# Roots and masks of the scale blocks on GpSimd in a four-layer graph network

## The chip, the cores and the metric

The kernel runs on one NeuronCore of one Trainium2 chip. The metric is the device time of one execution in microseconds (us), the median of several runs. The core has a matrix engine (TensorE, PE in the profile), a vector engine (VectorE, DVE), an engine for activation functions (ScalarE, ACT), a programmable vector engine (GpSimd, POOL) and a queue that issues the transfers (SyncE, SP). Each engine works through its own instructions in order and waits on semaphores for the others.

## The reference

The input is 64 graphs of 256 nodes with 128 features, x of shape (64, 256, 128), and a symmetric 0/1 adjacency with a diagonal of ones, adj of shape (64, 256, 256), in float32. Four layers follow each other, each with a residual and a norm over the features:

```
x = layernorm(x + L0(x, adj))   # max over neighbours j of relu(p_i + q_j + b)
x = layernorm(x + L1(x, adj))   # elu projections, aggregated by adj and adj^T, tanh
x = layernorm(x + L2(x, adj))   # graph convolution, see below
x = layernorm(x + L3(x, adj))   # see below
```

Two places have inverse roots beside the norms. Layer 2 scales the adjacency by the degrees:

```
A_hat = adj + eye;  deg = A_hat.sum(-1);  dinv = where(deg > 0, rsqrt(deg), 0)
norm_A = dinv[:, None] * A_hat * dinv[None, :]
```

Layer 3 normalizes a message for each pair of nodes, so it has one inverse root per pair:

```
pre = m_j[None, :] + m_i[:, None] + b1                       # (i, j, feature)
msg = gelu((pre - mean) * rsqrt(var + 1e-5) * g1 + be1)      # mean, var over features
agg = (msg * adj[i, j]).sum(j)
updated = layernorm(concat(x, agg) @ W2 + b2) * g2 + be2
```

## The kernel before, in words

The work is written as generators, one set per graph. Four stages of four neighbouring graphs run together: `last` of one graph (layer 3's messages and update), `third` of the next (layer 2, and the start of layer 3), `second` (layer 1) and `first` (sorting of the edges, layer 0). `together` takes turns among the four generators: each `yield` ends a turn, and the stages have weights of 34, 34, 14 and 44 turns. All 64 graphs are unrolled. The tile framework gives each instruction a place on its engine's queue from this order and from its own plan of when operands and buffers are free, so the order on a queue is near to the order in the code, not equal to it. The transfers all go through SP's queue.

Layer 3 works on edges alone. The edges of a graph, sorted into 40 slots, are laid out along the free dimension, features across the 128 partitions, in 10 tiles per graph of up to 1024 edges (eight of 1024, two of 704). `sums_of` makes one tile: matmuls into `bigp` (L728), the addition of the receiving node's part into `pre` (L732), the squares (L736, ACT), a matmul with ones for their sum over the features (L743), and the mean square plus eps as one row (L745, ACT). The row goes by DMA to a line in DRAM (L750). After every second tile, a group, the line is read back as a block `vr` of up to 128 partitions x 16 elements (L762), and a mask of the filled places as `fu` (L764); `inverse_root` makes 1/sqrt of the block (L74 on ACT, L75 on DVE), the mask is multiplied in (L769, DVE), and the block goes out to `scale_line` (L771). `last` fetches the scales of a tile two tiles ahead, broadcast to all partitions, as `rs_s` (L828), multiplies `pre` by them (L839, DVE), takes the Gelu (L841, ACT) and adds the message into the sums of the nodes (`fold`, L492). `sums_of` runs four tiles ahead of this.

There are 64 x 5 = 320 blocks `vr`. `inverse_root` serves two more places: `dinv` of layer 2, 128x2, once per graph (the degrees, L271 to L274; first used at L293), and `rs` of the norms, 128x2, five times per graph: in `layernorm` the variance plus eps (L174), a yield, the root, a yield, and the application (L180, or L184 and L185).

[...] an ACT_TABLE_LOAD stands before each change of set. Sqrt, Gelu (L841) and Exp (L194, L198, the elu) need different sets; squares, copies and the like need no load of their own.

Of the kernel before, what the change touches and what calls it, by code (L numbers as in the profile page):

```python
# [9 lines left out]
F32 = mybir.dt.float32  # L10
BF16 = mybir.dt.bfloat16
AF = mybir.ActivationFunctionType
ALU = mybir.AluOpType
# [6 lines left out]
P = 128  # L20
EPS = 1e-5
# [22 lines left out]
def kernel(  # L44
# [9 lines left out]
    nc = tc.nc  # L54
# [5 lines left out]
    consts = ctx.enter_context(tc.tile_pool(name="consts", bufs=1))  # L60
# [6 lines left out]
    eps_t = consts.tile([P, 1], F32, name="eps_t")  # L67
    nc.vector.memset(eps_t, EPS)
    minus1 = consts.tile([P, 1], F32, name="minus1")
    nc.vector.memset(minus1, -1.0)  # L70

    def inverse_root(t):

        nc.scalar.activation(t, t, AF.Sqrt)  # L74
        nc.vector.reciprocal(t, t)  # L75

    def load(src, shape, name):
        t = consts.tile(shape, F32, name=name)
# [43 lines left out]
    with tc.tile_pool(name="prep", bufs=1) as prep, tc.tile_pool(  # L122
        name="ps_prep", bufs=2, space=bass.MemoryType.PSUM
# [33 lines left out]
    class Shared:  # L157
# [5 lines left out]
        def psum(self):  # L163
            return self.ps_mm.tile([P, 512], F32, name="mm")

        def layernorm(self, dst, src, g=None, be=None):

            st = self.work.tile([P, H, 6], F32, name="st", bufs=4)
            mv = self.work.tile([P, H, 2], F32, name="mv", bufs=4)
            for h in range(H):  # L170
                nc.vector.bn_stats(st[:, h], src[:, h])
                nc.vector.bn_aggr(mv[:, h], st[:, h])
            rs = self.work.tile([P, H], F32, name="rs", bufs=4)
            nc.vector.tensor_scalar(rs, mv[:, :, 1], EPS, None, ALU.add)  # L174
            yield
            inverse_root(rs)
            yield
            for h in range(H):
                if g is None:
                    nc.vector.tensor_scalar(  # L180
                        dst[:, h], src[:, h], mv[:, h, 0:1], rs[:, h:h + 1], ALU.subtract, ALU.mult
                    )
                else:
                    nc.vector.scalar_tensor_tensor(dst[:, h], src[:, h], mv[:, h, 0:1], g, ALU.subtract, ALU.mult)  # L184
                    nc.vector.scalar_tensor_tensor(dst[:, h], dst[:, h], rs[:, h:h + 1], be, ALU.mult, ALU.add)  # L185
# [75 lines left out]
        def layer_2(self, s, aT, deg_of):  # L261
# [8 lines left out]
            dinv = work.tile([P, H], F32, name="dinv")  # L270
            nc.vector.tensor_scalar(dinv, deg, 1e-30, None, ALU.max)  # L271
            inverse_root(dinv)
            yield
            nc.vector.tensor_mul(dinv, dinv, pos)  # L274
# [79 lines left out]
    def sparse(ctx):  # L354
# [35 lines left out]
        with tc.tile_pool(name="cs_prep", bufs=1) as pp:  # L390
            t = pp.tile([P, P], F32, name="upto_f")
# [4 lines left out]
            t = pp.tile([P, N], I32, name="iota_i")  # L396
            nc.gpsimd.iota(t, pattern=[[1, N]], base=0, channel_multiplier=0)
            nc.vector.tensor_copy(iota_k, t)
            t = pp.tile([P, 1], I32, name="part_i")
# [25 lines left out]
            t = pp.tile([P, 1], F32, name="gbe")  # L425
# [9 lines left out]
            for i in range(3):  # L435
                t = pp.tile([3, P], BF16, name="u_part")
# [5 lines left out]
            t = pp.tile([ROWS, g_n, g_w], F32, name="tail_f")  # L442
# [15 lines left out]
        def pieces(lo, hi):  # L458

            for s0, n, w in RECTS:  # L460
                ss = [s for s in range(s0, s0 + n) if lo <= SLOT_AT[s][0] < hi]
                if ss:
                    assert SLOT_AT[ss[-1]][0] + w <= hi
                    yield ss[0], len(ss), w, SLOT_AT[ss[0]][0] - lo

        def block(ap, n, w, at):
            return ap[:, at:at + n * w].rearrange("p (s k) -> p s k", s=n)

        def widen(ap, n):

            return ap.unsqueeze(1).broadcast_to([ap.shape[0], n, ap.shape[1]])
# [246 lines left out]
        def sums_of(s, i):  # L718

            h, t0, tl = TODO[i]  # L720
            hot, c3, dT = s["hot"], s["c3"], s["dT"]
            pre = big.tile([P, TILE], F32, name="pre", bufs=7)
            s["pre", i] = pre
            for b in range(0, tl, 512):
                bl = min(512, tl - b)
                pt = ps_big.tile([P, 512], F32, name="bigp")
                for k in range(3):
                    nc.tensor.matmul(  # L728
                        pt[:, :bl], c3[:, k, h], hot[:, h, t0 + b:t0 + b + bl], start=k == 0, stop=k == 2
                    )  # L730
                for s0, n, w, at in pieces(t0 + b, t0 + b + bl):
                    nc.vector.tensor_add(  # L732
                        block(pre[:, b:], n, w, at), block(pt, n, w, at), widen(dT[:, h, :w], n)
                    )
            sq = big.tile([P, TILE], F32, name="sq", bufs=1)
            nc.scalar.activation(sq[:, :tl], pre[:, :tl], AF.Square)  # L736
            yield

            bl = P if tl % 512 == 0 else tl // 4
            v4 = sq[:, :tl].rearrange("p (b q k) -> p b q k", q=4, k=bl)  # L740
            pr = psum()
            for q in range(4):
                nc.tensor.matmul(pr[q * Q:(q + 1) * Q, :tl // 4], ones[:, :Q], v4[:, :, q], start=True, stop=True)  # L743
            row = big.tile([P, TILE // 4], F32, name="row")
            nc.scalar.activation(row[:, :tl // 4], pr[:, :tl // 4], AF.Identity, bias=eps_t, scale=1.0 / P)  # L745
            at = sum(n for _, _, n in TODO[i - i % GROUP:i])
            if at == 0:
                s["line"] = dram.tile([1, GROUP * TILE], F32, name="line")
            line = s["line"]
            nc.sync.dma_start(  # L750
                line[:, at:at + tl].rearrange("o (b q k) -> (o q) b k", q=4, k=bl),
                row.rearrange("(q p) n -> q p n", p=Q)[:, 0, :tl // 4].rearrange("q (b k) -> q b k", k=bl),
            )
            yield
            if i % GROUP < GROUP - 1:
                return

            n = at + tl
            rows = n // PIECE
            first_at = TODO[i - GROUP + 1][0] * WIDTH + TODO[i - GROUP + 1][1]  # L760
            vr = big.tile([P, PIECE], F32, name="vr")
            nc.sync.dma_start(vr[:rows], line[:, :n].rearrange("o (p k) -> (o p) k", k=PIECE))  # L762
            fu = big.tile([P, PIECE], BF16, name="fu")
            nc.sync.dma_start(  # L764
                fu[:rows],
                s["fulls"].rearrange("h w -> (h w)")[first_at:first_at + n].rearrange("(p k) -> p k", k=PIECE),
            )
            inverse_root(vr[:rows])
            nc.vector.tensor_mul(vr[:rows], vr[:rows], fu[:rows])  # L769
            out_line = dram.tile([1, GROUP * TILE], F32, name="scale_line")  # L770
            nc.sync.dma_start(out_line[:, :n].rearrange("o (p k) -> (o p) k", k=PIECE), vr[:rows])  # L771
            at = 0
            for j in range(i - GROUP + 1, i + 1):
                s["scale", j] = out_line[:, at:at + TODO[j][2]]
                at += TODO[j][2]
            yield
# [5 lines left out]
        def third(g, s):  # L782
# [35 lines left out]
            for i in range(AHEAD):  # L818
                yield from sums_of(s, i)

        def last(g, s):
# [11 lines left out]
            for i in range(len(TODO) + 1):  # L833
                if i < len(TODO):
                    if i + AHEAD < len(TODO):
                        yield from sums_of(s, i + AHEAD)
                    h, t0, tl = TODO[i]
                    pre, rs = s.pop(("pre", i)), scale_of.pop(i)
                    nc.vector.tensor_mul(pre[:, :tl], pre[:, :tl], rs[:, :tl])  # L839
                    msgs[i] = msg = pre if t0 else big.tile([P, TILE], F32, name="sums")  # L840
                    nc.scalar.activation(msg[:, :tl], pre[:, :tl], AF.Gelu, bias=be3, scale=g3)  # L841
                    fetch(i + 2)
                    yield
# [253 lines left out]
    with tc.tile_pool(name="flag", bufs=1) as fp, tc.tile_pool(  # L1097
        name="ps_flag", bufs=1, space=bass.MemoryType.PSUM
# [44 lines left out]
```

## Time and profile before

| what | before |
|---|---|
| median of 3 runs | 5732.73 us (5721.88 to 5733.99) |
| the profiled execution, its own time | 5731.62 us |
| its span, first to last instruction | 5729.7 us |
| TensorE's mean granted clock | 0.862 of full speed |
| busy: PE, DVE, ACT, POOL | 79%, 84%, 75%, 0% of the span |

The span is read from the trace of one execution; what lies around it is 1.9 us. Busy times count instructions in execution. A group row reads: line, engine, operation, output<-input tiles with shapes, count | busy us in all, mean ns of one | idle us of the engine just before them, and what ended most of it. The chain of waits is followed back from the last instruction, at each step to what released it.

### The profile page before, as it was taken

How to read it: one execution, taken by the hardware profiler on the slowest of the kernel's cores; microseconds unless marked ns; L12 is line 12 of the kernel's file. 1: busy time of each engine (PE TensorE's matmuls, PEld its weight loads, DVE VectorE, ACT ScalarE, POOL GpSimd, SP SyncE). 2: the span in 40 equal slices, each digit the busy share in tenths (PEclk: the TensorE clock that was granted, in tenths of full speed). 3: DMA queues.
4: the chain of work that ended last, by engine and by line, in shares of the span. 5: the costliest groups of instructions: out<-in, count | busy, mean ns of one | idle time of the engine just before them, and what ended most of it. 6: DMA issues, size and time to landing. Idle time of an engine off the chain costs nothing.

```text
span 5729.7 us, 83531 instructions
## 1 busy us (share of the span) xinstructions
PE 4529.9 (79%) x27408; PEld 2508.7 (44%) x27408; DVE 4834.4 (84%) x14654; ACT 4275.2 (75%) x6485; POOL 1.9 (0%) x10
## 2 busy tenths in 40 slices
PE   5878878878778778788788788787887887877875
PEld 2444444444444444444444444444444444444443
DVE  6788888888888888888888888888888888888876
ACT  2577777777777777777777777777777777777785
POOL 0000000000000000000000000000000000000000
PEclk8888889889889889888898898898888887888986
DMA  0122222222212221221221222122212212221222
GB/s 22 44 70 63 62 63 72 62 63 66 69 57 70 65 63 63 72 63 62 63 72 62 63 65 70 59 68 65 63 62 72 64 62 63 69 66 60 68 65 74
DMA packets 292813, 365.15 MB, mean 64 GB/s; under 512 B 151952, under 2 KB 210448, under 8 KB 292368
## 3 DMA queue, kind: packets, MB, share of 16 engines
q1 hardware_dynamic: 292368, 359.73, 20.0%
q8 instruction: 217, 3.56, 0.3%
q14 instruction: 228, 1.87, 0.1%
HBM read 345.07 MB, written 14.53 MB: 63 GB/s over the span
## 4 chain that ended last, share of the span: by engine, by line
PE 52%; DVE 29%; ACT 11%; issue 4%; DMA 3%; SPq 0%; DVEq 0%; POOL 0%; ACTq 0%
PE bigp L665 11%; PE bigp L728 8%; DVE pre L839 6%; PE mm L860 5%; DVE lanes L492 4%; PE mm L743 4%; DVE hot L629 4%; DVE pre L732 4%; DVE sums L492 3%; PE bigp L681 3%; DMA rs_s<-scale_line 2%; PE mm L870 2%; PE mm L296 2%; PE mm L699 2%; PE mm L647 2%
## 5 line engine op out<-in xcount | busy, mean ns | idle before, releaser
L665 PE MATMUL bigp<-hot,q 128*128 128x512 fp8e4 (+1 forms) x3840 | 1052.3, 371 | 66.6 <-DVE lanes L492 52.6
L728 PE MATMUL bigp<-hot,c 128*128 128x512 fp8e4 (+1 forms) x3840 | 928.8, 372 | 140.2 <-DVE pre L732 140.2
L732 DVE TENSOR_TENSOR pre<-bigp,dT 128x512 f32<-128x512 f32 (+6 forms) x1664 | 846.3, 530 | 37.8 <-PE bigp L728 33.5
L492 DVE TENSOR_TENSOR lanes<-bigp,lanes 128x512 f32<-128x512 f32 (+6 forms) x1536 | 772.7, 503 | 94.6 <-PE bigp L681 86.9
L839 DVE TENSOR_TENSOR pre<-pre,rs_s 128x1024 f32<-128x1024 f32 (+1 forms) x640 | 732.9, 1150 | 48.6 <-DMA rs_s<-scale_line 48.0
L736 ACT ACTIVATE sq<-pre 128x1024 f32<-128x1024 f32 (+1 forms) x640 | 638.5, 998 | 169.9 <-DVE pre L732 163.9
L841 ACT ACT_TABLE_LOAD x535 | 686.4, 1283 | 9.5
L492 DVE TENSOR_TENSOR sums<-pre,sums 128x1024 f32<-128x1024 f32 (+6 forms) x1024 | 628.8, 614 | 41.2 <-ACT pre L841 40.7
L745 ACT ACTIVATE row<-mm,eps_t 128x256 f32<-128x256 f32 (+1 forms) x640 | 289.6, 453 | 476.9 <-PE mm L743 476.7
L841 ACT ACTIVATE pre<-pre,be,g 128x1024 f32<-128x1024 f32 (+1 forms) x512 | 594.2, 1172 | 57.8 <-DVE pre L839 53.0
L743 PE MATMUL mm<-sq,ones 128*32 128x256 f32 (+1 forms) x5120 | 482.9, 440 | 135.2 <-ACT sq L736 135.2
L74 ACT ACT_TABLE_LOAD x445 | 570.9, 1283 | 7.5
L728 PEld LDWEIGHTS <-c 128*128 128x128 bf16 x3840 | 331.2, 98 | 550.5 <-issue 136.1
L665 PEld LDWEIGHTS <-q 128*128 128x128 bf16 x3840 | 310.8, 97 | 392.6 <-issue 112.0
L296 PE MATMUL mm<-aT,hs 128*128 128x256 f32 x512 | 232.3, 600 | 316.1 <-DVE hs L293 214.8
L629 DVE TENSOR_SCALAR hot<-rank 128x512 fp8e4<-128x512 bf16 (+5 forms) x1536 | 440.5, 348 | 0.0
L681 PEld LDWEIGHTS <-pick 42*128 42x128 bf16 x2944 | 155.8, 95 | 481.5 <-issue 474.2
L296 PEld LDWEIGHTS mm<-aT,hs 128*128 128x128 f32 x512 | 135.6, 293 | 425.8 <-issue 316.1
L860 PE MATMUL mm<-w3u,sums 128*128 128x128 f32 x2048 | 296.7, 289 | 18.4 <-DVE sums L492 16.1
L194 ACT ACT_TABLE_LOAD x221 | 283.5, 1283 | 3.9
L681 PE MATMUL bigp<-lack,pick 42*128 42x36 bf16 (+16 forms) x2944 | 285.7, 187 | 0.0
L860 PEld LDWEIGHTS mm<-w3u,sums 128*128 128x128 f32 x2048 | 254.5, 195 | 37.3 <-issue 17.6
(226 smaller groups left out, 7132.6 us busy)
## 6 DMA issues: line engine op xcount, KB each, us to landing
rs_s<-scale_line SPq DMA_DIRECT2D x512, 512.0 KB
rs_s<-scale_line SPq DMA_DIRECT2D x128, 352.0 KB
an<-in_adj SPq DMA_DIRECT2D x64, 256.0 KB
x<-in_x SPq DMA_DIRECT2D x64, 128.0 KB
line<-row SPq DMA_DIRECT2D x512, 4.0 KB
out<-o SPq DMA_DIRECT2D x64, 128.0 KB
fu<-fulls SPq DMA_DIRECT2D x192, 4.0 KB
vr<-line SPq DMA_DIRECT2D x192, 8.0 KB
```

The lines of the kernel that those rows point to most:

```text
L74: nc.scalar.activation(t, t, AF.Sqrt)
L492: nc.vector.tensor_tensor(lanes[:, :k, :w], src[:, i:i + k], lanes[:, :k, :w], op)
L629: nc.vector.tensor_scalar(hot[:, :, at:at + w], rank[:, :, :w], s0 + i + 1.0 - FAR, None, ALU.is_equal, saturate=False)
L665: nc.tensor.matmul(pt[:, :tl], q3[:, i, h], hot[:, h, t0:t0 + tl], start=i == 0, stop=False)
L681: nc.tensor.matmul(o_, l_, r_, start=False, stop=i == len(todo) - 1)
L728: nc.tensor.matmul(pt[:, :bl], c3[:, k, h], hot[:, h, t0 + b:t0 + b + bl], start=k == 0, stop=k == 2)
L732: nc.vector.tensor_add(block(pre[:, b:], n, w, at), block(pt, n, w, at), widen(dT[:, h, :w], n))
L736: nc.scalar.activation(sq[:, :tl], pre[:, :tl], AF.Square)
L743: nc.tensor.matmul(pr[q * Q:(q + 1) * Q, :tl // 4], ones[:, :Q], v4[:, :, q], start=True, stop=True)
L839: nc.vector.tensor_mul(pre[:, :tl], pre[:, :tl], rs[:, :tl])
L841: nc.scalar.activation(msg[:, :tl], pre[:, :tl], AF.Gelu, bias=be3, scale=g3)
L860: nc.tensor.matmul(pt[:, cols], lanes[:, k, cols], w3u[:, 1], start=k == 0, stop=False)
```

## The change

A constant `mhalf` of 128x16 elements of -0.5 is added. `inverse_root` becomes one instruction on GpSimd: the tile to the power of `mhalf`, in place. It now serves `vr` and `dinv` only. The mask of the `vr` block is multiplied in on GpSimd, too. The mask of `dinv` (L274) stays on DVE. In `layernorm` the root stays on ACT and takes eps as its bias, so the addition of eps on DVE goes; the reciprocal on DVE now stands after the second yield, ahead of the application.

```diff
+    mhalf = consts.tile([P, 16], F32, name="mhalf")
+    nc.vector.memset(mhalf, -0.5)
+
     def inverse_root(t):
 
-        nc.scalar.activation(t, t, AF.Sqrt)
-        nc.vector.reciprocal(t, t)
+        nc.gpsimd.tensor_tensor(t, t, mhalf[:t.shape[0], :t.free_size()], ALU.pow)
...
                 nc.vector.bn_stats(st[:, h], src[:, h])
                 nc.vector.bn_aggr(mv[:, h], st[:, h])
+            yield
             rs = self.work.tile([P, H], F32, name="rs", bufs=4)
-            nc.vector.tensor_scalar(rs, mv[:, :, 1], EPS, None, ALU.add)
-            yield
-            inverse_root(rs)
-            yield
+            nc.scalar.activation(rs, mv[:, :, 1], AF.Sqrt, bias=eps_t)
+            yield
+            nc.vector.reciprocal(rs, rs)
...
             inverse_root(vr[:rows])
-            nc.vector.tensor_mul(vr[:rows], vr[:rows], fu[:rows])
+            nc.gpsimd.tensor_mul(vr[:rows], vr[:rows], fu[:rows])
```

## The prediction

> **What bounds the kernel now.** No engine is full. I read the page first, from the engines' busy time to the chain of waits and the costliest groups:
>
> ```profile
> PE 4529.9 (79%) x27408; PEld 2508.7 (44%) x27408; DVE 4834.4 (84%) x14654; ACT 4275.2 (75%) x6485; POOL 1.9 (0%) x10
> ...
> PE 52%; DVE 29%; ACT 11%; issue 4%; DMA 3%; SPq 0%; DVEq 0%; POOL 0%; ACTq 0%
> ...
> L841 ACT ACT_TABLE_LOAD x535 | 686.4, 1283 | 9.5
> ...
> L74 ACT ACT_TABLE_LOAD x445 | 570.9, 1283 | 7.5
> ...
> L194 ACT ACT_TABLE_LOAD x221 | 283.5, 1283 | 3.9
> ```
>
> The first line has busy us, share and count: three engines at 75 to 84%, GpSimd (POOL) idle. The second is the chain that ended last: PE half, DVE 29%, ACT 11%. So the three hand work to each other in a fixed order, and relief on one counts only where the chain passes it. The last three rows are ACT's loads of function tables: 535 before a Gelu, 445 before a root, 221 before an Exp; with 32 of L198 and three others 1236 loads, 1586 us, over a third of ACT's busy time.
>
> Then the groups by shape, for all that the diff touches:
>
> ```profile
> L74 ACT ACTIVATE rs<-rs 128x2 f32<-128x2 f32 x320 | 64.4, 201 | 87.9 <-DVE rs L174 85.8
> ...
> L174 DVE TENSOR_SCALAR rs<-mv 128x2 f32<-128x2 f32 x320 | 51.1, 160 | 0.1
> ...
> L75 DVE RECIPROCAL vr<-vr 128x16 f32<-128x16 f32 x192 | 47.3, 246 | 27.9 <-ACT vr L74 23.9
> ...
> L74 ACT ACTIVATE vr<-vr 128x16 f32<-128x16 f32 x192 | 40.5, 211 | 3.7 <-DMA vr<-line 2.8
> ...
> L769 DVE TENSOR_TENSOR vr<-vr,fu 128x16 f32<-128x16 f32 x192 | 31.9, 166 | 0.2
> ...
> L75 DVE RECIPROCAL vr<-vr 108x16 f32<-108x16 f32 x128 | 31.2, 243 | 1.6 <-ACT vr L74 1.5
> ...
> L74 ACT ACTIVATE vr<-vr 108x16 f32<-108x16 f32 x128 | 27.6, 216 | 1.4
> ...
> L769 DVE TENSOR_TENSOR vr<-vr,fu 108x16 f32<-108x16 f32 x128 | 21.0, 164 | 0.1
> ```
>
> These are cheap one by one. The dear part of a root is the table load ahead of it, and the reload behind.
>
> Last the list of waits, and that of the DMA queue (us, times, longest):
>
> ```profile
> DVE pre L839 <- DMA rs_s<-scale_line: 48.0, 57, 4.2
> ...
> DVE vr L75 <- ACT vr L74: 25.4, 37, 1.7
> ```
> ```profile
> SPq L771 <- DVE vr L769: 565.2, 101, 7.6
> ```
>
> The scales of a block go line, vr, root, mask, scale_line, rs_s. Whoever needs them (L839) waited for them 57 times in 640, 48 us in all: the way has slack. From the timeline, the issue of vr to the issue of the scale_line store takes 5.7 us on average, 4.4 of it until ACT begins the root. There are 320 groups, one per 17.5 us (a graph takes 87.5 us in the middle of the span).
>
> [...] around 2822 us a load starts 0.01 to 0.02 us after the instruction ahead and the next one 1.30 us after it. I use 1283. [...]
>
> **The change, part by part.**
>
> ACT loses 320 vr roots (40.5 + 27.6 = 68 us) and 64 dinv roots (64 x 0.203 = 13 us). For the loads I listed ACT's instructions in the order of the timeline and counted one wherever the set changes (Tanh being in the sets of Exp and Gelu): this gives 535 + 445 + 255 = 1235 of the 1236 there. Without these 384 roots, the same count gives 379 + 195 + 192 = 766. So some 470 fewer, x 1.283 = 603 us. The norms' roots now take eps as a bias; [...] (L745 with bias 465 ns, L692 without 366, both 128x256 from PSUM): 320 x 0.093 = +30 us. ACT: -68 - 13 - 603 + 30 = -654, to 3621 us (63%).
>
> DVE loses the adds of L174 (51.1), the reciprocals of vr (78.5) and of dinv (64 x 0.146 = 9), and the masks (52.9): -192 us, to 4642. The reciprocal of rs stays, behind the step's yield, which can only let other DVE work go first. One memset is added, once.
>
> GpSimd gets 384 powers and 320 multiplications. Lower bound of a power: its own rows of before, 0.10 us for a memset of one element and 0.45 for an affine_select of 42x192, so at least about 0.15. Upper: 17 us, where it would fill the time of a group. [...] I take 0.5 to 1 us for the likeliest case and keep the rest for the range; that is a choice, not a derivation. The multiplication I put at 0.2, between the same rows.
>
> SP's queue keeps its order of DMAs: vr (L762), fu (L764), the store (L771), the fetch (L828). Their number is unchanged. L771 now waits for GpSimd, and behind it in SP stand line<-row and rs_s. The slot of fu is freed by GpSimd's multiplication. The way of the scales gets shorter while power and mask take under about 2.8 us (5.7 less the DMA's 2.9, the shortest start of the root after the issue). On GpSimd a dinv power can stand behind a vr power whose DMA isn't there; the cover is a step's yield and the transposes and matmul ahead of L293. I put that at nothing; without the cover, 64 x some 2 us.
>
> **What of it lies on the path.** I added up the chain's pieces over the span. Root loads of L74 48.1 us in 38 pieces; next to them are 38 vr roots (7.6 us), 8 of rs and 2 of dinv, so I count four fifths of these loads for vr: -38, and -8 for the roots. Reciprocal of vr 22.0, mask 10.0: both go. L174 22.1: goes. Exp loads 89.4 + 39.7, of which 255 to 192 takes a quarter: -32. Gelu loads 12.8, 29% fewer: -4. Sum: 38 + 8 + 22 + 10 + 22 + 32 + 4 = **-136 us**. Most of ACT's 654 us lies beside other work.
>
> Not all of it comes through: PE has 52% of the chain, and what is late next is PE's own matmuls at a granted clock of 0.862. I take two thirds: -91. Against it, GpSimd's holds: I laid a hold on DVE's timeline at each vr root, and let the next two-input instruction wait for its end. A hold of 0.5 us costs DVE 48 us in all, 1 us 154, 2 us 462, 3 us 781. DVE has 1681 us of its 4834 on the chain, 35%. The likeliest case with 0.5 us and a part of the rest: 48 x 0.35 = 17, and 2 for the shorter holds of the masks: +19. Sum -72 on the profiled execution's own 5731.6 us (span 5729.7 and 1.9 around it); the median of the runs is 1.1 higher. That gives **5660 us**. Own range 5605 (all of the 136) to 5715 (a fifth of it).
>
> **Rivals.** First, the other side: **GpSimd holds the read port that VectorE needs**, at L839 (640 instructions, 733 us), the sums of L492 (1024, 629 us), L201 and the residual adds. For: DVE is the fullest engine, two-input work is about a third of its time and often queued, and nothing on its side can move away. Against: 16 elements are little to read, and the port may be let go early. Price: a power of 3 us and a mask of 0.5 cost DVE 781 + 48 = 829 us, x 0.35 = +290, less 91: +199, **5931**. It decides from where the stall is 91 / 0.35 = 260 us, a power of about 1.3 us.
>
> Second, **the power is so slow that scales come late**: at 8 us the way grows by some 6 us. If one wait per graph takes that, 64 x 6 = 384, less 91: **6025**. Against: the slack at L839.
>
> Third, **nothing comes through**: PE's throttle takes back what PE gains from waiting less, or the reordered queues lose it. Then 5725 to 5740. For: a mean clock of 0.862, in records of 1.0 and 0.5 only, means half clock for (1 - 0.862) / 0.5 = 28% of the time.
>
> That the roots don't leave ACT at all can be excluded: the diff names the engine. That the loads stay can't: norms' roots could fall where the vr roots were, one load each; at most 320 root loads instead of 195, with as many reloads, takes 250 of the 470 away and leaves the path 30 to 40 us less gain: 5695.
>
> **Chances.** Likeliest case, the loads' rival included: 0.48. Nothing: 0.11. Port: 0.31. Late scales: 0.10. About 0.2% (11 us) is what a measurement of this kernel can tell from no change. Faster 0.48, same 0.11, slower 0.41. The range goes from 5600 to 5950: the likeliest case, no change, and the port up to a power of 3 us; what is left out is the late scales, some longer holds, and a gain beyond the 136 us.
>
> **What would show it.** Right: some 770 table loads, ACT near 3620 us, DVE near 4640 with L839 still at 1216 ns and the 128x1024 sums at 1219, no vr on the chain, few waits of L771 on POOL. Wrong: two-input DVE rows grown while PSUM rows (L732, 679 ns) stay, or idle DVE time at them: the port. L839 waiting for rs_s far over 48 us: late scales. Both absent and the span unchanged: PE, with a clock below 0.862.

## The result, and the profile after

| | before | after |
|---|---|---|
| median | 5729.0 us (5721.9 to 5734.0, 4 runs) | 5932.4 us (5931.3 to 5938.1, 4 runs) |
| ratio, with 95% interval | | 1.0358 (1.034 to 1.0376) |
| the profiled execution, its span | 5729.7 us | 5929.5 us |
| granted TensorE clock | 0.862 | 0.842 |
| table loads on ACT | 1236 | 765 |
| L841's (before: L839's) wait for rs_s | 48.0 us, 57 times | 630.2 us, 137 times |

The change makes the kernel 203 us slower, 3.6%. The page of the kernel after, from its busy line, its chain and its costliest groups (line numbers are 2 or 3 higher than before):

```profile
PE 4581.4 (77%) x27408; PEld 2517.9 (42%) x27408; DVE 4706.0 (79%) x13631; ACT 3681.2 (62%) x5630; POOL 1244.0 (21%) x714
...
issue 56%; POOL 17%; PE 13%; DMA 5%; DVE 5%; ACT 2%; SPq 1%; POOLq 0%; DVEq 0%; ACTq 0%
...
L77 POOL TENSOR_TENSOR vr<-vr,mhalf 128x16 f32<-128x16 f32 (+1 forms) x320 | 1006.4, 3145 | 4463.6 <-DMA vr<-line 4463.6
L841 DVE TENSOR_TENSOR pre<-pre,rs_s 128x1024 f32<-128x1024 f32 (+1 forms) x640 | 735.1, 1149 | 630.5 <-DMA rs_s<-scale_line 630.2
...
L843 ACT ACT_TABLE_LOAD x378 | 485.0, 1283 | 6.6
```

ACT went down as intended, and the shares of PE and VectorE fell, too: all three wait more. A power takes 3.1 us. Over half of this chain is "issue", time for which the profile shows no wait, so its shares aren't laid beside those of before; the rows and the waits carry the reading. GpSimd's groups by shape:

```profile
L77 POOL TENSOR_TENSOR vr<-vr,mhalf 128x16 f32<-128x16 f32 x192 | 591.7, 3082 | 2390.6 <-DMA vr<-line 2390.6
...
L771 POOL TENSOR_TENSOR vr<-vr,fu 128x16 f32<-128x16 f32 x192 | 102.8, 536 | 15.1
L771 POOL TENSOR_TENSOR vr<-vr,fu 108x16 f32<-108x16 f32 x128 | 90.7, 708 | 10.0
L77 POOL TENSOR_TENSOR dinv<-dinv,mhalf 128x2 f32<-128x2 f32 x64 | 44.7, 698 | 149.1 <-DVE dinv L273 149.0
```

The records of GpSimd fit together: in all 320 blocks the mask begins 0.08 us after the power ends, and the store is issued 0.03 us after the mask ends. The list of waits, and under it the DMA queue's own (us in total, times, longest):

```profile
DVE pre L841 <- DMA rs_s<-scale_line: 630.2, 137, 6.9
...
DVE dinv L276 <- POOL dinv L77: 142.1, 61, 4.1
```
```profile
SPq L773 <- POOL vr L771: 1713.0, 320, 9.1
```

The last row isn't to be laid beside the 565.2 us that the prediction quotes, which is one releaser of several: before, SP stood at this store for 1251 us in all, 259 times.

The wait for the scales has grown by 582 us, and nearly all of it lies at two of the ten tiles of a graph: the third (312.9 us in 63 graphs) and the fifth (298.9 us in 63), each the first tile of its block. That is 5.0 and 4.7 us per graph. A second wait is new: VectorE's mask of the degrees (L276) waits 2.3 us, 61 times, for their power.

Two rows of VectorE decide on the first rival, that GpSimd holds VectorE up. Before:

```profile
L839 DVE TENSOR_TENSOR pre<-pre,rs_s 128x1024 f32<-128x1024 f32 x512 | 622.3, 1216 | 22.8 <-DMA rs_s<-scale_line 22.2
...
L492 DVE TENSOR_TENSOR sums<-pre,sums 128x1024 f32<-128x1024 f32 x256 | 312.0, 1219 | 37.0 <-ACT pre L841 36.9
```

And after:

```profile
L841 DVE TENSOR_TENSOR pre<-pre,rs_s 128x1024 f32<-128x1024 f32 x512 | 621.9, 1215 | 331.5 <-DMA rs_s<-scale_line 331.2
...
L494 DVE TENSOR_TENSOR sums<-pre,sums 128x1024 f32<-128x1024 f32 x256 | 311.2, 1216 | 49.2 <-ACT pre L843 49.0
```

Both have two inputs in SBUF, and take as long as before. In the trace, 70 of these 768 instructions lie wholly inside a power, with a mean of 1218 ns. So VectorE isn't locked out by a power. It is GpSimd's instructions that take longer where the two meet. A stretch of the timeline (start, duration, both in us):

```profile
2913.02 1.21 DVE L841 TENSOR_TENSOR pre<-pre,rs_s 128x1024 f32<-128x1024 f32 x1
...
2913.29 3.71 POOL L77 TENSOR_TENSOR vr<-vr,mhalf 128x16 f32<-128x16 f32 x1 [12.41 <-DMA vr<-line]
...
2917.07 1.34 POOL L771 TENSOR_TENSOR vr<-vr,fu 128x16 f32<-128x16 f32 x1
2917.12 1.21 DVE L494 TENSOR_TENSOR sums<-pre,sums 128x1024 f32<-128x1024 f32 x1
...
2918.44 0.32 SPq L773 DMA_DIRECT2D scale_line<-vr  x1
...
2923.80 1.23 DVE L841 TENSOR_TENSOR pre<-pre,rs_s 128x1024 f32<-128x1024 f32 x1 [4.55 <-DMA rs_s<-scale_line]
```

The power began while L841 ran and took 3.71 us where the shortest take 2.90. The mask met the sums of L494 and took 1.34 us where the shortest take 0.22. Then the store, the fetch, and VectorE stands 4.55 us at the next L841. Over the trace a mask that meets no multiplication of L841 and no addition into the sums takes 0.25 us on average (188), one that meets one 1.10 us (132); a power takes 2.91 us (130) and 3.30 us (190).

### The profile page after: what moved, and what is told of

Same layout as the page of the kernel before. It is cut to its first block, busy times and chain, and to the rows that moved or that the text cites. A ratio compares the mean times of both kernels' runs of the same rounds, so it can differ in the third digit from the quotient of the medians.

```text
span 5929.5 us, 82239 instructions
## 1 busy us (share of the span) xinstructions
PE 4581.4 (77%) x27408; PEld 2517.9 (42%) x27408; DVE 4706.0 (79%) x13631; ACT 3681.2 (62%) x5630; POOL 1244.0 (21%) x714
## 4 chain that ended last, share of the span: by engine, by line
issue 56%; POOL 17%; PE 13%; DMA 5%; DVE 5%; ACT 2%; SPq 1%; POOLq 0%; DVEq 0%; ACTq 0%
POOL vr L77 14%; PE bigp L667 5%; POOL vr L771 3%; DMA rs_s<-scale_line 2%; PE bigp L730 2%; DMA vr<-line 2%; PE bigp L683 1%; DVE pre L841 1%; DMA line<-row 1%; PE mm L862 1%; PE mm L745 1%; POOL dinv L77 1%; PE mm L812 1%; PE mm L701 1%; DVE lanes L494 0%
## 5 line engine op out<-in xcount | busy, mean ns | idle before, releaser
L77 POOL TENSOR_TENSOR vr<-vr,mhalf 128x16 f32<-128x16 f32 (+1 forms) x320 | 1006.4, 3145 | 4463.6 <-DMA vr<-line 4463.6
L841 DVE TENSOR_TENSOR pre<-pre,rs_s 128x1024 f32<-128x1024 f32 (+1 forms) x640 | 735.1, 1149 | 630.5 <-DMA rs_s<-scale_line 630.2
L730 PE MATMUL bigp<-hot,c 128*128 128x512 fp8e4 (+1 forms) x3840 | 940.7, 378 | 171.1 <-DVE pre L734 159.8
L494 DVE TENSOR_TENSOR lanes<-bigp,lanes 128x512 f32<-128x512 f32 (+6 forms) x1536 | 772.9, 503 | 148.9 <-PE bigp L683 144.6
L734 DVE TENSOR_TENSOR pre<-bigp,dT 128x512 f32<-128x512 f32 (+6 forms) x1664 | 831.4, 528 | 13.3 <-PE bigp L730 5.6
L494 DVE TENSOR_TENSOR sums<-pre,sums 128x1024 f32<-128x1024 f32 (+6 forms) x1024 | 626.5, 612 | 52.6 <-ACT pre L843 52.1
L745 PE MATMUL mm<-sq,ones 128*32 128x256 f32 (+1 forms) x5120 | 470.9, 446 | 197.6 <-ACT sq L738 197.6
L667 PEld LDWEIGHTS <-q 128*128 128x128 bf16 x3840 | 291.9, 98 | 402.0 <-DVE q L501 103.5
L298 PE MATMUL mm<-aT,hs 128*128 128x256 f32 x512 | 259.3, 661 | 186.7 <-DVE hs L295 186.7
L568 PE MATMUL mm<-perm,nz 128*128 128x256 bf16 x256 | 74.6, 377 | 373.8 <-DVE perm L562 373.8
L298 PEld LDWEIGHTS mm<-aT,hs 128*128 128x128 f32 x512 | 149.6, 323 | 305.1 <-issue 273.6
```

What stands on the lines that cost most here:

```text
L77: nc.gpsimd.tensor_tensor(t, t, mhalf[:t.shape[0], :t.free_size()], ALU.pow)
L494: nc.vector.tensor_tensor(lanes[:, :k, :w], src[:, i:i + k], lanes[:, :k, :w], op)
L667: nc.tensor.matmul(pt[:, :tl], q3[:, i, h], hot[:, h, t0:t0 + tl], start=i == 0, stop=False)
L730: nc.tensor.matmul(pt[:, :bl], c3[:, k, h], hot[:, h, t0 + b:t0 + b + bl], start=k == 0, stop=k == 2)
L734: nc.vector.tensor_add(block(pre[:, b:], n, w, at), block(pt, n, w, at), widen(dT[:, h, :w], n))
```

## The experiments

Each run is set against runs of the kernel before on the same chip (medians 5728 to 5730 us).

| run | median us | ratio to before, 95% interval |
|---|---|---|
| e1 power as multiplication | 5629.0 | 0.9826 (0.9809 to 0.9842) |
| e2 a second power as mask | 6589.7 | 1.1505 (1.1486 to 1.1524) |
| e3 blocks back on ACT and DVE | 5804.9 | 1.0136 (1.0119 to 1.0153) |
| e4 norms' edit alone | 5807.9 | 1.0136 (1.0119 to 1.0153) |
| e5 powers, norms as before | 5919.9 | 1.0341 (1.0324 to 1.0358) |
| e6 after, five tiles ahead | 5965.3 | 1.0413 (1.0396 to 1.0431) |
| e7 after, blocks of 128x8 | 5648.5 | 0.9856 (0.9840 to 0.9873) |
| e8 eps as bias alone | 5814.8 | 1.0155 (1.0138 to 1.0172) |
| e9 before, blocks of 128x8 | 5974.7 | 1.0433 (1.0416 to 1.0450) |
| e10 as e7, power as multiplication | 5470.6 | 0.9553 (0.9537 to 0.9569) |
| e11 blocks of 128x8, powers, norms as before | 5549.9 | 0.9690 (0.9674 to 0.9706) |
| e12 as e5, power as multiplication | 5661.8 | 0.9888 (0.9871 to 0.9904) |

**Is it the power's duration, or the new order of the queues?** e1 and e2 leave the order alone.

```diff
-    nc.vector.memset(mhalf, -0.5)
+    nc.vector.memset(mhalf, 0.0039)
...
-        nc.gpsimd.tensor_tensor(t, t, mhalf[:t.shape[0], :t.free_size()], ALU.pow)
+        nc.gpsimd.tensor_tensor(t, t, mhalf[:t.shape[0], :t.free_size()], ALU.mult)
```

> The 384 powers are multiplications by 0.0039, so neither the roots nor the values of the output are computed; every queue holds the same instructions in the same order as the changed kernel. Theory A (the power's 2.9 us stand in the way of the scales, and the order of the queues was planned for a short instruction): the block's root falls to about 0.2 us, L841's wait for rs_s from 630 to under 100 us, time 5600 to 5700. Theory B (the new order of the queues itself is bad, whatever the power takes): 5850 to 5940, with L841's wait still over 400 us. Theory C (GpSimd holds VectorE's port): falls too, but through shorter two-input rows on DVE, not through L841's wait.

```diff
-            nc.gpsimd.tensor_mul(vr[:rows], vr[:rows], fu[:rows])
+            nc.gpsimd.tensor_tensor(vr[:rows], vr[:rows], fu[:rows], ALU.pow)
```

> The mask is applied as an exponent (power in place of a multiplication), so a masked scale is 1, not 0; same order on every queue as the changed kernel, with a second power of some 2.9 us in each of the 320 groups. Theory A: the way of the scales is 2.5 us longer, two waits per graph grow by it and further tiles begin to wait: 64 x 2 x 2.5 = 320 us or more, time 6200 to 6400. Theory B: within 30 us of 5932. Theory C: up as well, by at most the 320 x 2.5 us that DVE is locked out, and the two-input rows of DVE grow by several hundred us.

GpSimd's row and the waits of e1:

```profile
L77 POOL TENSOR_TENSOR vr<-vr,mhalf 128x16 f32<-128x16 f32 x192 | 79.3, 413 | 2760.3 <-DMA vr<-line 2760.3
```
```profile
DVE pre L841 <- DMA rs_s<-scale_line: 275.2, 127, 5.2
...
DVE dinv L276 <- POOL dinv L77: 3.6, 6, 0.9
```

And those of e2:

```profile
L771 POOL TENSOR_TENSOR vr<-vr,fu 128x16 f32<-128x16 f32 x192 | 618.5, 3222 | 15.1
```
```profile
DVE pre L841 <- DMA rs_s<-scale_line: 1052.6, 203, 9.5
...
DVE dinv L276 <- POOL dinv L77: 262.0, 62, 6.4
```

In the traces of e1 and e2 every engine's instructions follow each other as in the kernel after. A multiplication of 0.4 us in the place of a power of 3.1 us gives 5629, and a power of 3.2 us in the place of a mask of 0.6 us gives 6590. Theory A holds, and B falls as the cause of the loss. From e1 to after the median rises by 303 us, 4.7 us per graph; the wait for the scales rises by 355 us and that for the degrees by 138, other waits of VectorE fall, and its idle time rises by 333 us in all. From after to e2 the median rises by 657 us, 10.3 per graph, more than was expected: beside the third and the fifth tile (305 us more) the ninth of each graph begins to wait (111.7 us), and the degrees stand behind two powers (120 us more). e1 also lets other values flow than the kernel after; in e2 only the masked scales differ, and it moves the same way. Theory C falls with the rows of VectorE above: in e2, with GpSimd busy for 2080 us, L841 at 128x1024 took 1218 ns. That one order serves both operations also shows that the planner gave the power no longer a place than a multiplication. e1 still has 275 us of the wait for the scales, where Theory A expected under 100: the order is tight even for a short root.

The traces show how tight. Call lead the time from the issue of a block's `vr` to the first multiplication that needs the block, less the wait there; the way begins at the same issue, and the part of it that the power is in ends at the issue of the store. Means over the 64 graphs, in us:

| | before | e1 | after | e2 |
|---|---|---|---|---|
| second block: lead | 12.3 | 7.5 | 7.6 | 7.7 |
| issue of `vr` to issue of the store | 4.9 | 3.2 | 6.8 | 9.5 |
| wait at the third tile | 0.0 | 1.4 | 4.9 | 7.4 |
| third block: lead | 12.5 | 7.2 | 7.2 | 7.2 |
| issue of `vr` to issue of the store | 5.9 | 4.1 | 6.3 | 8.6 |
| wait at the fifth tile | 0.4 | 2.8 | 4.7 | 6.9 |

The lead is some 5 us shorter in the new order, and the same in all three runs of it, whatever the power takes and however long SP stands at the store (829 us in e1, 2523 in e2). With the lead fixed, the wait grows as the way does.

**The edits apart.** e3 puts the blocks back (root on ACT, reciprocal and mask on DVE), e4 the degrees as well.

> The blocks' roots, reciprocals and masks are back on ScalarE and VectorE; the power of the degrees stays on GpSimd and the norms' edit stays. Theory A: the loss goes, 5690 to 5740. If the norms' edit or the degrees' power cost time, it stays above 5760. Table loads should be near 1236 again, less a few.

> Only the norms' edit: eps as the bias of the root on ScalarE, the addition on VectorE gone, the reciprocal behind the second yield; blocks and degrees as before. Expected 5690 to 5735: 51 us of DVE additions go, of which 22 us were on the chain. Against the kernel with the degrees on GpSimd as well, the difference is what 64 powers of 128x2 (0.70 us each) cost: -10 to +30 us.

Both missed: 5805 and 5808. They agree with each other, and in e3 VectorE waits for the powers of the degrees twice, 1.1 us in all: with no block's power ahead of them they are not in the way. As a price of these powers the agreement is weak, since e3 also has 122 table loads fewer than e4 (1146 against 1268). The norms' edit alone costs 78 us (e4 and e8 also keep the constant `mhalf`, unused; what that makes isn't separated). e8 takes the norms' edit apart, e5 leaves it out of the changed kernel:

```diff
             rs = self.work.tile([P, H], F32, name="rs", bufs=4)
-            nc.vector.tensor_scalar(rs, mv[:, :, 1], EPS, None, ALU.add)
             yield
-            inverse_root(rs)
+            nc.scalar.activation(rs, mv[:, :, 1], AF.Sqrt, bias=eps_t)
+            nc.vector.reciprocal(rs, rs)
             yield
```

> The kernel before with eps as the root's bias in place of the addition on VectorE, and the reciprocal right behind the root, ahead of the second yield, as before. If the reciprocal's new place made the loss of the norms' edit alone (5808), this is at 5700 to 5735; if the bias or the missing addition makes it, by the new order that the plan gives, it is near 5808.

> The changed kernel with the norms as before (addition of eps on VectorE, root and reciprocal together, then the yield); blocks and degrees keep their powers on GpSimd. Theory A (the power in the way of the scales makes the loss): still well above before, 5830 to 5950, with L841 waiting several hundred us. If the norms' edit makes a loss of its own (its run alone took 78 us more than before) that adds to it: about 5932 - 78 = 5854. If the queues' order matters most, anything from 5650 to 5950.

The place of the reciprocal is not it: e8 is at 5815. In e4 and e8 the queues are ordered anew; ACT has 1268 table loads in both instead of 1236. In the changed kernel the same edit costs 12 us (5932 against 5920). With short roots it gains 33, as e12 shows:

> As the run with the norms as before and powers on GpSimd (5920), its powers being multiplications by 0.0039, so the roots of blocks and degrees aren't computed; same order on every queue as that run. Theory A: the power's duration costs as much here as with the norms' edit, where it was 303 us: 5600 to 5640.

e12 is at 5662, 258 us under e5 with the same order, so a second order confirms the price of the power (expected were 5600 to 5640). And with e1 at 5629, the norms' edit has no fixed sign: 78, 12, -33 us. That it acts through the order that comes out is likely, but not shown; which place in the order makes the 78 us stays open.

**More lead, or a shorter way.** e6 changes `AHEAD` from 4 to 5, with 8 buffers of `pre` and 2 of `rs_s`.

> The changed kernel with tiles made five ahead instead of four (pre has 8 buffers, rs_s 2 instead of 3 to make room), so a block of scales is begun one tile earlier. Theory A: the waits at L841 for the scales fall from 630 to under 200 us, time 5640 to 5740. If the two buffers of rs_s hold the fetches up, or the order is at fault, it stays above 5800.

It is slower still, 5965, where Theory A expected 5640 to 5740. The wait for the scales did fall, from 630 to 378 us (under 200 was expected), but the order changed: 883 table loads instead of 765 (118 x 1.283 = 151 us of ACT), and powers of 128x16 that take 3.78 us on average. Whether the order or the two buffers of `rs_s` hold it up isn't separated. e7 makes the way shorter instead, with shorter powers and with no tile that waits for the second of a pair; the shares of the two aren't separated:

```diff
-        GROUP = 2
-        PIECE = 16
+        GROUP = 1
+        PIECE = 8
```

> The changed kernel with one tile to a block of scales instead of two, laid out as 128x8: 640 powers of 8 elements per partition. From the rows of the changed kernel (2.90 us for 16, 0.70 us for 2) a power of 8 should take 1.64 us; there are 3 x 320 more small transfers on SP. Theory A: the first tile of a pair doesn't wait for the second, and the way is 1.3 us shorter: waits at L841 under 300 us, time 5680 to 5800. Against it: the transfers delay each other in SP's queue, then 5900 and more.

> The kernel before with one tile to a block of scales (128x8), roots and masks on ScalarE and VectorE: the control for the changed kernel with such blocks (5648). 320 more roots, reciprocals and masks (some 0.21 + 0.23 + 0.16 us each) and up to 320 more pairs of table loads. If the smaller blocks alone made the gain, 5640 to 5700; if they help only because the power on GpSimd is shorter and begins sooner, this is slower than before, 5760 to 5900.

> The changed kernel with blocks of 128x8 and the powers as multiplications by 0.0039, so the roots aren't computed; same order on every queue as the run with blocks of 128x8 and powers (5648). It shows what 1.4 us per power still cost there. Theory A: the wait of L841 (249 us) mostly goes, 5500 to 5600. If the powers are hidden in this order, 5640 to 5650.

GpSimd's row and the wait of e7:

```profile
L77 POOL TENSOR_TENSOR vr<-vr,mhalf 128x8 f32<-128x8 f32 x512 | 962.7, 1880 | 2879.9 <-DMA vr<-line 2879.9
```
```profile
DVE pre L841 <- DMA rs_s<-scale_line: 248.8, 192, 5.1
```

The shortest power of eight elements takes 1.63 us (1.64 was worked out), the mean 1.9 us. The changed kernel gains 284 us by it, more than was expected, and is 1.4% faster than before. The same blocks with roots on ScalarE (e9) lose 4.3%, also more than was expected: 1409 table loads, ACT busy for 4524 us. So the small blocks alone don't make the gain; they pay here together with roots that need no table load. e10 shows what the powers cost even so: 178 us, with the wait down to 46.1 us without them.

> Blocks of 128x8 with powers and masks on GpSimd, the norms as before. In the changed kernel the norms' edit made 12 us (5932 against 5920 without it); so 5630 to 5670 here. In the kernel before, it made 78 us by another order of the queues; a difference of that size would again be the order.

e11 is the best version that computes everything: 5549.9 us, 3.1% faster than before. It missed the 5630 to 5670 that were expected: with these blocks the norms as before gain 99 us on e7. Another order has come out (683 table loads instead of 766); whether that is the whole of it isn't shown. Against e9, which has the same blocks and the same norms, the roots and masks on GpSimd gain 425 us. The busy line and the wait of e11:

```profile
PE 4381.6 (79%) x27408; PEld 2410.7 (43%) x27408; DVE 4745.6 (86%) x13951; ACT 3519.2 (63%) x5548; POOL 1534.5 (28%) x1354
```
```profile
DVE pre L842 <- DMA rs_s<-scale_line: 278.4, 165, 5.8
```

## Why the prediction was wrong

- **What is taken away was sized well.** 766 table loads forecast, 765 there. In the trace of before all 1236 loads stand at the first Gelu or where Sqrt, Gelu, Exp and Tanh change from one to another; none stands at the 431 repeats of one of them, nor where Tanh follows Gelu (61 times) or Exp (once). ACT -654 us forecast; the durations of its instructions add up to 648 us less. DVE -192 us forecast, 208 less in the same sum. The bias made a norm's root 93 ns longer (294 ns against 201), the 0.093 us that it was priced at; the two rows named beside that price, of L745 and L692, differ by 99 ns. The busy times fell by only 594 and 128 us, because busy time counts the overlap of neighbours once and there is less of it after. What came through to the end was taken as -91 us; e1, with a short instruction for the root, measures -101. That these two agree is in part luck: e1 contains 275 us of waits for the scales, which the -91 left out.
- **The step that failed is the duration of the power.** "I take 0.5 to 1 us for the likeliest case", the text says. It is 2.9 us at least and 3.1 on average. The text had bounds of 0.15 and 17 us and no row between; the value taken was near the lower one, and its price in the sum was +17 us, as a hold on VectorE. That a power holds VectorE was the author's assumption; no trace shows it. Measured, the power's duration costs 303 us (e1 against after), more than everything that was gained.
- **The second failed step is the slack.** "The way has slack", from 48 us of waits at L839. This is slack in the order of before, and the diff makes a new order, in which two of a graph's five blocks have 7 to 8 us of lead instead of 12 to 13. That is why the wait grew thirteenfold although the issue of `vr` to the issue of the store went from 5.69 to only 6.29 us on average over all blocks (the root starts 2.4 us after the issue, no longer 4.4), and why e1, with 3.52 us, still waits 275 us. After, the second block's scales are there 12.5 us after the issue of its `vr`; with the lead of before the wait would have been some 0.2 us in place of 4.9, an estimate from these averages. By it, the waits for the scales need both, the slow power and the shorter lead. `AHEAD` = 5 (e6) raised the two leads to 8.3 and 9.3 us only. What in the plan makes them shorter stays open.
- **A reading was off, without making the loss.** 2.9 us was taken for the shortest start of the root after the issue of `vr`, and power and mask were allowed 2.8 us. The trace of before has starts at 1.53 and 1.62 us, and GpSimd's shortest after is 1.49 us, so there was more room than was thought.
- **The degrees.** Put at nothing, with "64 x some 2 us" if the cover is gone: it was gone, with 142 us. In e1, where the power ahead is short, it is 3.6 us.
- **The first rival names 5931 us and the runs 5932: a coincidence.** Its power of 3 us and mask of 0.5 were near what was measured, its mechanism was not. The read port that it names was an assumption, shown in no trace: VectorE's two-input rows are unchanged (1215 and 1216 ns against 1216 and 1219), and the delays fall on GpSimd, in the way of the scales (a mask takes 1.10 us where it meets such an instruction and 0.25 elsewhere, a power 3.30 and 2.91).
- **The second rival, late scales, is what happened**, at 3.1 us and not 8. It was given 0.10, and its threshold was worked out from the slack above.
- **The third rival, PE's throttle, did not take the gain back.** e1 is faster at a clock of 0.865, e11 at 0.888. After, the clock is lower than before (0.842 against 0.862); how much of the 203 us goes with that isn't separated.
- **The form of the forecast.** Faster was given 0.48 and slower 0.41. The range, 5600 to 5950, reached to what came because the rivals' ends were kept in it; the forecast of 5660 has the wrong sign. The range of the likeliest case, 5605 to 5715, comes out of its terms only with half of the 19 us of holds, which it doesn't say.

## What to carry to other kernels

Before work goes to an idle engine, bound the duration of the new instruction there; if no row shows it, measure it alone. Here the elements per partition set it (at the shortest 2.90 us for 128x16 and for 108x16, 1.63 us for 128x8), so a block may be cut smaller for the new engine. An instruction off all busy engines can still lie in a chain that others wait on, and waits found in the old order of the queues don't bound those in a new one. Compare the lead between the two orders, then hold the order still and swap a long operation for a short one of the same form, and the price of its duration shows by itself.

## What the runs showed of the hardware that was not expected

- A float32 power with tensor exponents on GpSimd takes, at the shortest, 2.90 us for 128x16, 1.63 us for 128x8, and 0.70 us for 128x2. An estimate from these three: some 0.16 us per element of a partition and 0.4 us on top. A multiplication of the same 128x16 takes 0.22 us at the shortest.
- A mask on GpSimd that meets a multiplication of L841 or an addition into the sums takes 1.10 us on average (132), one that meets none 0.25 us (188). The order of the two doesn't decide it: in 56 of the 132 meetings the mask's record begins first, yet the mask takes 1.26 us on average there. VectorE's side shows no such delay: the 70 instructions of 128x1024 that ran wholly inside a power took 1218 ns on average, against 1216 and 1219 ns in the rows of before.
- The granted clock of the profiled execution is mostly higher in the kernels of lower median: 0.824 at 6590 us, 0.842 at 5932, 0.862 at 5729, 0.865 at 5629, 0.888 at 5550, but 0.875 at 5471. Whether it is cause or effect, no run here separates.
